# Moving the checks of sums and small norm steps from GpSimd to VectorE, and the bias add into an accumulating DMA

## The chip, the cores and the metric

The kernel runs on one core of a Trainium2 chip. The metric is the device time of one execution in microseconds (us). The engines are PE (TensorE, matmuls), DVE (VectorE), ACT (ScalarE), POOL (GpSimd) and SP (SyncE); each works through its own instructions in program order and waits for others through semaphores. DMAs are issued from SP and from POOL.

## The reference

Two layers of a transformer over graphs with 16 graphs (b), 1024 nodes and 256 features. Each layer computes h = relu(layernorm(x)), then masked attention over h, and adds the result to x. The first layer has 4 heads of 64, the second 8 heads of 32 and biases on its projections:

```python
h = jnp.maximum(_layernorm(x, axis=-1), 0.0)
scores = jnp.einsum('bhne,bhme->bhnm', Q, K) * scale
scores = jnp.where(mask, scores, -jnp.inf)
attn = jax.nn.softmax(scores, axis=-1)
heads = jnp.einsum('bhnm,bhme->bhne', attn, V)
x = x + concat @ Wo.T + bo
```

The mask comes from an integer adjacency matrix of 1024 x 1024 for each b. All arithmetic is float32.

## The kernel before, in words

The whole work of both layers is one stream of steps, whose order is written out by the program itself. A layer of one b has two halves of 512 query rows (qh) and two groups of heads (g) in each; a group is 4 steps in the first layer and 8 in the second, so that there are 768 steps in all. The first layer of element b+1 stands in the stream ahead of the second layer of element b. A step computes four blocks of scores, 128 keys by 512 queries each, in two PSUM pairs of tiles: `scores` (PE, L372); then for each pair the mask is put on by a minimum (DVE, L388) and the exponential is taken (ACT, L393). Two steps later `weigh` multiplies with the values (PE, L405). Three PSUM pairs are shared by the scores, the projections (`kq` L212, `values` L241), the transposes (`turn` L200) and the output projection (`end_half` L353).

The sums of the exponentials are formed in two ways. In the first layer, `add_tiles` adds a step's tiles on DVE or POOL (L416) and to the running sum on POOL (L418). In the second layer, POOL adds the tiles of two successive steps in place (`count_steps`, L502). A matmul with ones (L278) then sums over the keys.

After the last step of a group its sums go through a fixed set of calls that are due some steps later. `spread` brings them by two small DMAs into `sn`, a tile of 128 lanes by 8 (first layer) or 16 elements. `invert` takes the reciprocal on DVE (L305) and brings it back by DMAs as `inv`. `test`, one step after `invert`, checks on POOL that each sum lies between 1e-15 and 1e15 and multiplies the outcome into the tile `chk` (L318, L319). `normalize` multiplies on POOL (L324), and `end_half` projects and adds to x (DVE, L358). At the end of the program `chk` decides whether a slower, careful program has to run.

The norms are prepared beside the stream: `stats` takes mean and variance on DVE (L165, L166), then four small POOL operations give `rstd` and `shift` (L169 to L175); `norm` applies them on ACT (L182); `add_bias`, a step after the last part of `norm`, adds the output bias `bo` to the rows of x on POOL (L190), long before `end_half` adds the projected attention to the same rows. The functions due in a step are called after that step's exponentials, so that on DVE and POOL they stand between the masking of this step and that of the next; those in the set LARGE and `turn` come last. The adjacency rows are loaded by casting DMAs that POOL issues (L126), transposed by SP's DMAs (L130), and changed in place on DVE for the second layer (`second`, L144).

Of the kernel before, what the change touches and what calls it, by code (L numbers as in the profile page):

```python
# [10 lines left out]
F32 = mybir.dt.float32  # L11
# [4 lines left out]
ALU = mybir.AluOpType  # L16
PSUM = bass.MemoryType.PSUM

P = 128
EPS = 1e-5  # L20
# [62 lines left out]
def fast_program(ctx, tc, a, w, loads, chk):  # L83
# [3 lines left out]
    nc = tc.nc  # L87
    x, adj, out = a["x"], a["adj"], a["out"]
    B, N, E = x.shape
# [8 lines left out]
    small = ctx.enter_context(tc.tile_pool(name="small", bufs=4))  # L98
# [50 lines left out]
    class Inputs:  # L149
# [6 lines left out]
        def stats(self, half, tiles=range(4)):  # L156
            n = f"{self.n}_{half}"
            if 0 in tiles:
                self.mv[half] = small.tile([P, 4, 2], F32, tag="mv", name=f"mv_{n}")
            mv = self.mv[half]  # L160
            for i in tiles:
                stats = small.tile(
                    [P, nc.vector.BN_STATS_DIM], F32, tag="stats", name=f"st_{n}_{i}"
                )
                nc.vector.bn_stats(stats, xs[self.b, half][:, i, :])  # L165
                nc.vector.bn_aggr(mv[:, i, :], stats)  # L166
            if 3 in tiles:
                ve = small.tile([P, 4], F32, tag="ve", name=f"ve_{n}")
                nc.gpsimd.tensor_scalar_add(ve, mv[:, :, 1], EPS)  # L169
                self.rstd[half] = small.tile([P, 4], F32, tag="rstd", name=f"rstd_{n}")  # L170
                nc.gpsimd.tensor_tensor(self.rstd[half], ve, w.mhalf, ALU.pow)
                less = small.tile([P, 4], F32, tag="less", name=f"less_{n}")
                nc.gpsimd.tensor_scalar_mul(less, mv[:, :, 0], -1.0)
                self.shift[half] = small.tile([P, 4], F32, tag="shift", name=f"shift_{n}")
                nc.gpsimd.tensor_mul(self.shift[half], less, self.rstd[half])  # L175

# [10 lines left out]
        def add_bias(self, half):  # L187

            rows = xs[self.b, half]
            nc.gpsimd.tensor_add(  # L190
                rows, rows, w.bo[self.layer].unsqueeze(1).to_broadcast([P, 4, E])
            )

        def turn(self, half):
# [56 lines left out]
    class Group:  # L251
# [62 lines left out]
        def test(self):  # L314
            c = chk[:, : self.n_f]
            for bound, op in ((SUM_MIN, ALU.is_ge), (SUM_MAX, ALU.is_le)):
                ok = small.tile([P, self.n_f], F32, tag="ok", name=f"ok_{self.n}_{op.name}")
                nc.gpsimd.tensor_scalar(ok, self.sn, bound, 1.0, op0=op, op1=ALU.mult)  # L318
                nc.gpsimd.tensor_mul(c, c, ok)  # L319

        def normalize(self):
            if self.g == 0:
# [301 lines left out]
    for b in range(B - 1):  # L624
        mine, a, c = inputs[1][b], first[b + 1], second[b]
# [284 lines left out]
```

## Time and profile before

| | |
|---|---|
| Median of 3 runs (lowest to highest) | 3377.39 us (3377.24 to 3378.44) |
| The profiled execution, its span | 3380.06 us, 3378.3 us |
| Granted TensorE clock | 0.998 |
| Busy: PE, DVE, POOL, ACT | 99%, 74%, 72%, 65% |
| DMA queue of POOL: packets, MB, share of 16 engines | 18432, 33.56, 6.3% |
| DMA queue of SP | 232080, 105.18, 12.6% |

A line of the timeline has the start in us, the length in us, the engine, the line of the kernel, the operation and the tiles that it writes and reads, and in brackets the idle time of the engine just before it with what ended it; neighbours of one kind are merged, and x counts them. A line of the groups has the busy time in us, the mean length in ns, and the idle time before. The ends of matmuls are modelled, so PE is better read from the starts of its instructions.

### The profile page before, as it was taken

The page shows a single profiled execution, that of the slowest core. Times are in us where ns is not written, and L with a number is a line of the kernel's source. Part 1 is how long each engine was busy: PE and PEld are TensorE (multiplying, and loading weights), DVE is VectorE, ACT ScalarE, POOL GpSimd, SP SyncE. Part 2 cuts the span into 40 slices and gives each one's busy share as a digit, 9 for nine tenths or more (in the row PEclk, how much of TensorE's full clock was granted, in tenths as well). Part 3 has the DMA queues.
Part 4 walks back from the last instruction along what each step waited for, and adds up shares of the span by engine and source line. Part 5 has one row for each costly group of instructions (what it writes and reads, how often), then busy time and mean ns, then how long its engine had stood idle before and what let it go on. Part 6 is the DMA issues. An engine that isn't in the chain of part 4 may idle for free. (4 is left out here: it accounts for less than half of the span.)

```text
span 3378.3 us, 46298 instructions
## 1 busy us (share of the span) xinstructions
PE 3339.0 (99%) x18190; PEld 1298.6 (38%) x18190; DVE 2501.1 (74%) x2664; ACT 2182.5 (65%) x2402; POOL 2447.1 (72%) x1606
## 2 busy tenths in 40 slices
PE   8999999999999999999999999999999999999998
PEld 3443333333333333333334333333343333433432
DVE  4676767767677786777867778677786777777876
ACT  5567566675666756667566675666756667665665
POOL 5577778777677766877677686777867778676776
PEclk9999999999999999999999999999999999999999
DMA  6221111212112111121221212212121111210001
GB/s 131 48 42 36 48 39 36 51 36 47 36 36 51 42 42 36 39 48 42 45 39 36 48 39 48 39 39 45 39 47 37 48 39 36 51 38 18 14 17 31
DMA packets 250738, 141.77 MB, mean 42 GB/s; under 512 B 182416, under 2 KB 217488, under 8 KB 250512
## 3 DMA queue, kind: packets, MB, share of 16 engines
q1 hardware_dynamic: 232080, 105.18, 12.6%
q0 software_dynamic: 18432, 33.56, 6.3%
q8 instruction: 144, 2.36, 0.3%
q14 instruction: 82, 0.67, 0.1%
HBM read 120.33 MB, written 18.34 MB: 41 GB/s over the span
## 5 line engine op out<-in xcount | busy, mean ns | idle before, releaser
L393 ACT ACTIVATE p<-p 128x1024 f32<-128x1024 f32 x1536 | 1615.1, 1057 | 973.8 <-DVE p L388 931.7
L388 DVE SCALAR_TENSOR_TENSOR p<-mask,ps 128x1024 f32<-128x1024 fp8e4 x1536 | 1797.0, 1215 | 583.5 <-PE ps L372 553.8
L502 POOL TENSOR_TENSOR p<-p,p 128x2048 f32<-128x2048 f32 x255 | 1161.9, 4557 | 372.2 <-PE po L405 368.3
L372 PE MATMUL ps<-qT,kT 32*128 32x512 f32 (+1 forms) x6144 | 1145.6, 631 | 7.6 <-DVE p L388 4.9
L405 PE MATMUL po<-p,v 128*32 128x512 f32 (+1 forms) x6144 | 992.4, 601 | 0.4 <-ACT o L288 0.4
L418 POOL TENSOR_TENSOR t<-t,t 128x1024 f32<-128x1024 f32 x192 | 486.2, 2532 | 389.8 <-DVE t L416 341.6
L372 PEld LDWEIGHTS ps<-qT,kT 32*128 32x128 f32 (+1 forms) x6144 | 367.7, 184 | 675.7 <-issue 305.3
L405 PEld LDWEIGHTS po<-p,v 128*32 128x32 f32 (+1 forms) x6144 | 227.8, 118 | 689.4 <-issue 529.1
L416 DVE TENSOR_TENSOR t<-p 128x1024 f32<-128x1024 f32 x192 | 325.0, 1693 | 14.6 <-POOL t L418 14.4
L278 PE MATMUL pz<-p,ones 128*32 128x512 f32 x2056 | 267.8, 593 | 0.2 <-POOL p L502 0.2
L212 PE MATMUL pq<-hT,wk 128*128 128x512 f32 x512 | 240.7, 613 | 3.1 <-ACT hT L201 3.1
L353 PE MATMUL py<-wo,cat 128*128 128x256 f32 x1008 | 237.8, 387 | 4.7 <-POOL cat L324 2.8
L241 PE MATMUL pv<-wv,hT 128*128 128x256 f32 x1024 | 237.9, 385 | 0.1
L212 PE MATMUL pq<-hT,wq 128*128 128x512 f32 x512 | 236.6, 605 | 0.0
L241 PEld LDWEIGHTS pv<-wv,hT 128*128 128x128 f32 x1024 | 189.4, 190 | 71.7 <-issue 24.0
L353 PEld LDWEIGHTS py<-wo,cat 128*128 128x128 f32 x1008 | 185.4, 190 | 80.0 <-issue 33.4
L324 POOL TENSOR_TENSOR cat<-o,inv 128x512 f32<-128x512 f32 x127 | 164.5, 1296 | 10.3 <-DMA inv<-vd 9.3
L416 POOL TENSOR_TENSOR t<-p 128x1024 f32<-128x1024 f32 x64 | 165.0, 2578 | 2.8 <-ACT p L393 2.4
L358 DVE TENSOR_TENSOR x<-py,x 128x1024 f32<-128x1024 f32 x63 | 76.4, 1213 | 118.4 <-PE py L353 118.4
L190 POOL TENSOR_TENSOR x<-x,bo 128x1024 f32<-128x1024 f32 x64 | 152.6, 2385 | 1.5 <-DMA bo<-in_bo_dram 1.4
L212 PEld LDWEIGHTS pq<-hT,wk 128*128 128x128 f32 x512 | 93.5, 192 | 145.2 <-issue 120.1
L212 PEld LDWEIGHTS pq<-hT,wq 128*128 128x128 f32 x512 | 92.2, 189 | 139.8 <-issue 138.3
(51 smaller groups left out, 1635.4 us busy)
## 6 DMA issues: line engine op xcount, KB each, us to landing
adj<-in_adj_dram POOLq DMA_DIRECT2D x128, 256.0 KB, 3.6
x<-in_x_dram SPq DMA_DIRECT2D x32, 512.0 KB
inv<-vd SPq DMA_DIRECT2D x128, 128.0 KB
inv<-vd SPq DMA_DIRECT2D x252, 64.0 KB
out_dram<-x SPq DMA_DIRECT2D x31, 512.0 KB
adjT<-adj SPq DMA_TRANSPOSE x128
sd<-s SPq DMA_DIRECT2D x64, 4.0 KB
sn<-sd SPq DMA_DIRECT2D x64, 4.0 KB
```

Source lines behind the costliest of these rows:

```text
L212: nc.tensor.matmul(pq[:, m, :], wt[self.layer][:, c, ts(m, P)], self.hT[half][:, c, :], start=(c == 0), stop=(c == 1),)
L241: nc.tensor.matmul(pv[:, i, :], self.hT[half][:, c, ts(i, P)], w.v[self.layer][:, c, :], start=(c == 0), stop=(c == 1),)
L278: nc.tensor.matmul(self.s[r * self.D : (r + 1) * self.D, :], w.ones[:, : self.D], p[:, r, :], start=start, stop=stop,)
L324: nc.gpsimd.tensor_mul(self.half.cat[:, self.g, :], self.ob, self.inv)
L353: nc.tensor.matmul(py[:, i, :], self.half.cat[:, c, ts(i, P)], w.o[self.layer][:, c, :], start=(c == 0), stop=(c == 1),)
L372: nc.tensor.matmul(st.ps[i // 2][:, i % 2, :], gr.inp.kT[r * D : (r + 1) * D, gr.g, ts(kt, P)], gr.inp.qT[r * D : (r + 1) * D, gr.g, ts(gr ...
L388: nc.vector.scalar_tensor_tensor(out=half, in0=gr.mask.m[:, kt, ts(gr.qh, 512)].unsqueeze(1).to_broadcast([P, 2, 512]), scalar=BIG, in1=st ...
L393: nc.scalar.activation(half, half, AF.Exp, scale=gr.scale)
L405: nc.tensor.matmul(gr.o[r * D : (r + 1) * D, :], gr.inp.v[:, kt, h * D : (h + 1) * D], st.p[:, i, :], start=(kt == 0), stop=(kt == NT - 1),)
L416: engine.tensor_add(t, st.p[:, 0:2, :], st.p[:, 2:4, :])
L418: nc.gpsimd.tensor_add(t, t, gr.t)
L502: nc.gpsimd.tensor_add(one, one, st.p)
```

## The change

The four operations of `test` for a group become two on DVE, each of which compares `sn` with a bound and multiplies the outcome into `chk`; the tiles `ok` go. In `stats`, the addition of EPS and the negation of the mean go from POOL to DVE; the power and the product stay on POOL. In `add_bias`, POOL issues a DMA that adds the bias, repeated for four row tiles, to the rows of x in SBUF.

```diff
             if 3 in tiles:
                 ve = small.tile([P, 4], F32, tag="ve", name=f"ve_{n}")
-                nc.gpsimd.tensor_scalar_add(ve, mv[:, :, 1], EPS)
+                nc.vector.tensor_scalar_add(ve, mv[:, :, 1], EPS)
                 self.rstd[half] = small.tile([P, 4], F32, tag="rstd", name=f"rstd_{n}")
                 nc.gpsimd.tensor_tensor(self.rstd[half], ve, w.mhalf, ALU.pow)
                 less = small.tile([P, 4], F32, tag="less", name=f"less_{n}")
-                nc.gpsimd.tensor_scalar_mul(less, mv[:, :, 0], -1.0)
+                nc.vector.tensor_scalar_mul(less, mv[:, :, 0], -1.0)
...
         def add_bias(self, half):
 
             rows = xs[self.b, half]
-            nc.gpsimd.tensor_add(
-                rows, rows, w.bo[self.layer].unsqueeze(1).to_broadcast([P, 4, E])
+            nc.gpsimd.dma_start(
+                rows, w.bo[self.layer].unsqueeze(1).to_broadcast([P, 4, E]), accum_op=ALU.add
             )
...
         def test(self):
             c = chk[:, : self.n_f]
             for bound, op in ((SUM_MIN, ALU.is_ge), (SUM_MAX, ALU.is_le)):
-                ok = small.tile([P, self.n_f], F32, tag="ok", name=f"ok_{self.n}_{op.name}")
-                nc.gpsimd.tensor_scalar(ok, self.sn, bound, 1.0, op0=op, op1=ALU.mult)
-                nc.gpsimd.tensor_mul(c, c, ok)
+                nc.vector.scalar_tensor_tensor(
+                    out=c, in0=self.sn, scalar=bound, in1=c, op0=op, op1=ALU.mult
+                )
```

## The prediction

> **What bounds the kernel now.** I read the page's busy shares first, then the groups, then every gap between the starts of consecutive matmuls, then the timeline around the places where the moved instructions stand.
>
> ```profile
> PE 3339.0 (99%) x18190; PEld 1298.6 (38%) x18190; DVE 2501.1 (74%) x2664; ACT 2182.5 (65%) x2402; POOL 2447.1 (72%) x1606
> ...
> L502 POOL TENSOR_TENSOR p<-p,p 128x2048 f32<-128x2048 f32 x255 | 1161.9, 4557 | 372.2 <-PE po L405 368.3
> ...
> L416 DVE TENSOR_TENSOR t<-p 128x1024 f32<-128x1024 f32 x192 | 325.0, 1693 | 14.6 <-POOL t L418 14.4
> ...
> L190 POOL TENSOR_TENSOR x<-x,bo 128x1024 f32<-128x1024 f32 x64 | 152.6, 2385 | 1.5 <-DMA bo<-in_bo_dram 1.4
> ```
>
> PE is the bound, and not only by its modelled busy time. In the gaps between starts I find the same distance for the same pair of lines again and again, and an excess over it of 28.4 us in all: 11.4 before 100 us, 5.1 after 3200 us, and about 0.78 us in each of the 208.4 us periods between (one batch element each). So at most some 28 us can be gained, and in the steady state 0.78 a period. DVE and POOL have idle time but stand in strict order: what they delay reaches PE once its slack is gone.
>
> The second thing to see is that DVE and POOL exclude each other. The tensor_tensor of L416 has a mean of 1693 ns, though undisturbed it takes 1.22 us; here it starts during a POOL add:
>
> ```profile
> 420.32 2.38 POOL L416 TENSOR_TENSOR t<-p 128x1024 f32<-128x1024 f32 x1
> 420.48 3.32 DVE L416 TENSOR_TENSOR t<-p 128x1024 f32<-128x1024 f32 x1
> ```
>
> POOL ends at 422.70, DVE at 423.80: DVE waited for POOL's end and then took 1.1 us. And once, late in the run, such a wait reaches PE:
>
> ```profile
> 3211.27 4.54 POOL L502 TENSOR_TENSOR p<-p,p 128x2048 f32<-128x2048 f32 x1 [0.24 <-PE po L405]
> ...
> 3212.40 3.96 DVE L144 TENSOR_SCALAR mask<-mask 128x1024 fp8e4<-128x1024 fp8e4 x1
> ...
> 3216.28 3.47 DVE L388 SCALAR_TENSOR_TENSOR p<-mask,ps 128x1024 f32<-128x1024 fp8e4 x3
> ...
> 3217.55 1.13 PE L372 MATMUL ps<-qT,kT 32*128 32x512 f32 x4 [2.10 <-DVE p L388]
> ```
>
> L144 normally takes 0.69 us. Blocked by L502 until 3215.81 it takes 3.96, the masking L388 behind it is late, and PE stands still for 2.1 us.
>
> [...] L388 reads one SBUF tensor and PSUM, and its 1536 times lie between 1159 and 1224 ns. [...] Here the 256 KB adj DMAs occupy POOL for 527 to 773 ns and land after 3.6 us.
>
> **The change part by part.** POOL loses 64 x 2.385 us (L190), 256 small operations of L318 and L319 (some 1.25 us a group with gaps) and two small ones a norm. It gains 64 DMA issues. DVE gains two two-input operations a group (256) and two tensor_scalar a norm (128). I price each of these at 0.15 us, below the 0.17 to 0.25 us of the small reciprocal L305: 384 x 0.15 = 58 us of 877 us DVE idle time. As busy time this is nothing. What counts is that each check now waits on DVE for POOL's current instruction, with the L388 pair of the next step queued behind it, then ACT's exponentials and PE. I go through one period with DVE's order written out.
>
> Site A, second layer's second group, its check comes at 1146.96, right after the norm statistics:
>
> ```profile
> 1140.91 4.56 POOL L502 TENSOR_TENSOR p<-p,p 128x2048 f32<-128x2048 f32 x1 [3.95 <-PE po L405]
> ...
> 1145.41 0.59 POOL L126 DMA_DIRECT2D adj<-in_adj_dram  x1
> ...
> 1146.08 0.27 POOL L318 TENSOR_SCALAR ok_is_ge<-sn 128x16 f32<-128x16 f32 x1
> ...
> 1146.78 0.18 DVE L166 BATCH_NORM_AGGREGATE mv<-st 128x2 f32<-128x6 f32 x1
> 1146.88 2.33 DVE L388 SCALAR_TENSOR_TENSOR p<-mask,ps 128x1024 f32<-128x1024 fp8e4 x2
> ...
> 1147.27 4.55 POOL L502 TENSOR_TENSOR p<-p,p 128x2048 f32<-128x2048 f32 x1
> ...
> 1149.27 3.07 PE L241 MATMUL pv<-wv,hT 128*128 128x256 f32 x13
> ```
>
> With L318 and L319 off POOL, the next L502 starts at 1146.07 instead of 1147.27 (its inputs are ready: it overwrites a tile that PE read last by 1144.49) and ends at 1150.62. The check, ready at 1146.96, waits 3.7 us; with two operations of 0.15 the L388 pair is 4.0 late. That pair ends at 1149.21 and PE takes the freed PSUM pair at 1149.27: slack 0.06. PE loses 3.95 us. The place recurs 14 times: **55 us**.
>
> Site B, fourth group, check behind the L388 that ends at 1176.15:
>
> ```profile
> 1170.58 4.60 POOL L502 TENSOR_TENSOR p<-p,p 128x2048 f32<-128x2048 f32 x1
> ...
> 1173.79 4.62 DVE L388 SCALAR_TENSOR_TENSOR p<-mask,ps 128x1024 f32<-128x1024 fp8e4 x4 [1.51 <-PE ps L372]
> ...
> 1175.11 2.45 POOL L190 TENSOR_TENSOR x<-x,bo 128x1024 f32<-128x1024 f32 x1
> ```
>
> Before, L190 stands at 1168.26 and 1175.11, and L502 follows at 1178.84. If a bias DMA occupies POOL as an adj issue does (0.62 us), the first L502 starts at about 69.0, the second at 74.9 and blocks the check from 76.1 to 79.5: 3.7 us late, slack 1.67 (freed at 1177.28, used at 1178.94), 2.05 us lost, 14 times: **29 us**. If the issue takes over about 1.57 us the check slips in ahead: nothing. The trace has no accumulating DMA; 512 pieces of 1 KB against 128 rows of an adj load could cost up to four times 0.62, so the bounds are 0.6 and 2.5 us, and I take the low end.
>
> Site C, first layer's last group, 1076.50: L502 runs to 1079.62, DVE was idle until 1077.70 and has slack 1.71; 0.57 us, 14 times: **8**. Site D, 1063.49: two norm operations and two checks in a row, slack 0.2 after a gap of 0.2, and the pow L171 (1.04) may get in between: 0 to 1.3 us, I take 0.5, 14 times: **7**. The other tensor_scalar pairs: one meets an L502 for about 2.2 us with slack 1.73[...]: 0 to 0.6, I take 0.3: **4**. The remaining four checks of a period fall into DVE idle time of 1 to 5 us (at 1021, 1042, 1114, 1207): nothing; without that cover each could cost up to one POOL add, 2.4 or 4.6 us. After 3200 us, where L502 runs almost without pause, five checks lose about 2.2 each: **11**.
>
> POOL's relief brings: L324 is late for PE's L353 by 0.38 us once a period behind L318 and L319, with 0.16 at the next L372: 0.55, 15 times: **-8**. The opening norm chain may be 0.5 us shorter, or later if its order turns out worse; taken at nothing. Of the DMA: 33.5 MB more on a queue that now takes 6.3% of the engines; x is needed again many steps later (L358), which hides landing. It could slow the small transfers to sn, on which DVE waits 43.5 us in all: 0 to 14 us, taken at nothing because round trip and use are 1 to 3 us apart. POOL's pow now waits for DVE's ve; behind it stand L324 and L502, which mostly wait for PE anyway.
>
> Sum: 55 + 29 + 8 + 7 + 4 + 11 - 8 = 106 us. The profiled execution took 3380.06 (span 3378.3 and 1.8 around it), 2.7 above the median 3377.39; nothing in the difference matters at this size. 3377 + 106 = 3483, given as **3480**.
>
> **Rivals.** (1) The issue is long: site B goes, 3454. For it speak the 512 pieces; it is inside the main case. (2) The block is worse: second check also behind an add, D and the pairs at their high ends, shifted POOL adds meeting L416 and L144: some 40 us more, 3525. (3) No block for operations of 8 or 16 elements[...]: then only 0.3 us a period is added at A against 0.55 regained: 3374, no change. Against it speaks POOL's own L318 of 8 elements, which takes up to 1119 ns instead of 253 beside a DVE L416. (4) Faster: POOL's relief takes effect[...]. It decides at A, from a wait under 0.06 us: 8 us of the period stalls and up to 6 of the opening go: 3363. (5) The accumulation is carried out in more pieces or with a wait of POOL for its landing (3.6 us or more, 64 times): POOL would lose more than L190 costs, sites shift, 3400 to 3500.
>
> **How the numbers follow.** About 0.2% (6.8 us) is what a measurement of this kernel can tell from no change. Blocking, with or without site B, and (5): 0.88, all slower. No change: 0.07. Faster: 0.05. The range 3400 to 3525 runs from A at half its size with the gains to the high ends.
>
> **What would show it.** Right: the check's operations on DVE with a median near 0.15 us but a maximum of 3 to 4.6 us; L372 or L241 with idle time put down to L388; stalls of about 4 us every 208 us; DVE idle time down; POOL without L190. Wrong: maxima under 0.5 us, or an unchanged period of 208.4 us. A long POOL time for the bias DMA would show rival 1.

## The result, and the profile after

The changed kernel takes 3577.14 us (median of 4 runs, 3572.55 to 3577.28) against 3377.38 us: a ratio of 1.0587, interval 1.0569 to 1.0606, 200 us more. The forecast was 3480 us with a range up to 3525. The direction held, the size was about half. The profiled execution has a span of 3575.3 us, 197.0 more than before.

These lines of the profile after answer to those shown of before (three dots stand for lines left out). In a busy line each engine has its busy time, its share of the span and its number of instructions; a group has busy time, mean ns of one, and idle time before it with what ended it; a DMA issue has the KB of one and the us to landing.

```profile
PE 3435.9 (96%) x18190; PEld 1328.1 (37%) x18190; DVE 2762.4 (77%) x3048; ACT 2183.9 (61%) x2402; POOL 2192.2 (61%) x966
...
L502 POOL TENSOR_TENSOR p<-p,p 128x2048 f32<-128x2048 f32 x255 | 1175.7, 4611 | 633.9 <-PE po L405 617.6
L372 PE MATMUL ps<-qT,kT 32*128 32x512 f32 (+1 forms) x6144 | 1205.6, 644 | 104.1 <-DVE p L388 97.8
...
L416 DVE TENSOR_TENSOR t<-p 128x1024 f32<-128x1024 f32 x192 | 282.7, 1473 | 2.4 <-POOL t L418 2.0
...
L317 DVE SCALAR_TENSOR_TENSOR chk<-sn,chk 128x8 f32<-128x8 f32 (+1 forms) x256 | 242.6, 948 | 4.4
...
x<-bo POOLq DMA_DIRECT2D x64, 512.0 KB, 6.4
```

POOL lost 255 us of busy time, and gained as much idle time behind PE. The checks L317, 8 or 16 elements each, have a mean of 948 ns, 242.6 us in all. L372 now stands idle for 104.1 us, of which 97.8 were ended by the mask L388, which stands on DVE behind the checks. Before, it was 7.6 us in the whole run:

```profile
L372 PE MATMUL ps<-qT,kT 32*128 32x512 f32 (+1 forms) x6144 | 1145.6, 631 | 7.6 <-DVE p L388 4.9
```

The line of all checks together shows that the mean is made of two kinds (min/median/max):

```profile
L317 DVE SCALAR_TENSOR_TENSOR chk<-sn,chk x256: 134/174/3937, 90.5 to 3565.5; 128x8 f32<-128x8 f32 x64, 128x16 f32<-128x16 f32 x64
```

At site A the timeline runs as the forecast said. (Start and length in us; x2 merges the two checks.)

```profile
1192.71 0.58 POOL L126 DMA_DIRECT2D adj<-in_adj_dram  x1
...
1193.31 4.55 POOL L502 TENSOR_TENSOR p<-p,p 128x2048 f32<-128x2048 f32 x1
...
1194.18 3.93 DVE L317 SCALAR_TENSOR_TENSOR chk<-sn,chk 128x16 f32<-128x16 f32 x2
...
1198.03 2.35 DVE L388 SCALAR_TENSOR_TENSOR p<-mask,ps 128x1024 f32<-128x1024 fp8e4 x2
...
1199.30 2.08 PE L372 MATMUL ps<-qT,kT 32*128 32x512 f32 x4 [3.15 <-DVE p L388]
...
1201.31 5.30 PE L241 MATMUL pv<-wv,hT 128*128 128x256 f32 x16
```

L502 follows the adj issue at once, the checks become ready at 1194.18 and end with L502, and PE stands still until the mask is done. What the forecast did not have is in the last two lines. Before, four matmuls of L372 are shown with 1.13 or 1.14 us and 13 of L241 with 3.07; here four take 2.08 and 16 take 5.30. The starts of L241 lie 427 ns apart instead of 216. The windows give the reason: after the length of a window and the busy times of PE, PEld, DVE, ACT and POOL stands the granted TensorE clock, then the DMA share and GB/s.

```profile
1192.00:1199.00 7.00, 4.14 (x28) 1.03 (x26) 6.90 (x9) 2.12 (x2) 5.84 (x3) 0.91 0.53 112
1199.00:1206.00 7.00, 6.70 (x18) 4.40 (x19) 5.90 (x14) 4.23 (x4) 2.47 (x3) 0.61 0.00 0
1206.00:1212.00 6.00, 6.00 (x46) 2.05 (x45) 4.12 (x7) 3.98 (x6) 3.15 (x1) 1.00 0.01 3
```

From 1197.70 to 1204.53, for 6.83 us, the trace has the clock at one half; then it is full again. In the whole run such stretches last 184.9 us (32 of them, all but two of 3.41 or 6.83 us), before 16.9 us (3); the last one of each run reaches 2.0 us past the last instruction. The mean granted clock fell from 0.998 to 0.974.

Both kernels issue the same 18190 matmuls, in the same order but for four near the end, so each gap between two starts can be set against the same gap of before. The excess, summed by place, is split in two: what matmul work lost in half-clock stretches (half of their overlap), and the rest, which is standing still.

| Place (forecast's name) | forecast | standing still | half clock |
|---|---|---|---|
| A, second layer's second group, 14 times | 55 | 52.9 | 37.2 |
| B, its fourth group, 14 times | 29 | 35.1 | 12.6 |
| C, first layer's last group, 15 times | 8 | 16.2 | 2.9 |
| D | 7 | 1.8 | 0 |
| norms' tensor_scalars | 4 | 12.4 | 0 |
| after 3190 us | 11 | 25.0 | 13.3 |
| relief of POOL | -8 | -16.3 | 0 |
| opening and rest | 0 | 1.0 | 2.9 |
| sum | 106 | 128.1 | 68.9 |

The two measured columns make up the 197.0. (Where a stretch begins within a standstill the split is good to some us.)

### The profile page after: what moved, and what is told of

It is laid out like the page before. It is cut to its first block, busy times and chain, and to the rows that moved or that the text cites. A ratio compares the mean times of both kernels' runs of the same rounds, so it can differ in the third digit from the quotient of the medians.

```text
span 3575.3 us, 46236 instructions
## 1 busy us (share of the span) xinstructions
PE 3435.9 (96%) x18190; PEld 1328.1 (37%) x18190; DVE 2762.4 (77%) x3048; ACT 2183.9 (61%) x2402; POOL 2192.2 (61%) x966
## 3 DMA queue, kind: packets, MB, share of 16 engines
q0 software_dynamic: 52224, 67.12, 12.7%
## 5 line engine op out<-in xcount | busy, mean ns | idle before, releaser
L388 DVE SCALAR_TENSOR_TENSOR p<-mask,ps 128x1024 f32<-128x1024 fp8e4 x1536 | 1796.9, 1214 | 587.6 <-PE ps L372 586.8
L502 POOL TENSOR_TENSOR p<-p,p 128x2048 f32<-128x2048 f32 x255 | 1175.7, 4611 | 633.9 <-PE po L405 617.6
L372 PE MATMUL ps<-qT,kT 32*128 32x512 f32 (+1 forms) x6144 | 1205.6, 644 | 104.1 <-DVE p L388 97.8
L405 PE MATMUL po<-p,v 128*32 128x512 f32 (+1 forms) x6144 | 1006.0, 609 | 3.9 <-ACT p L393 3.3
L372 PEld LDWEIGHTS ps<-qT,kT 32*128 32x128 f32 (+1 forms) x6144 | 376.3, 186 | 809.1 <-issue 314.9
L416 DVE TENSOR_TENSOR t<-p 128x1024 f32<-128x1024 f32 x192 | 282.7, 1473 | 2.4 <-POOL t L418 2.0
L241 PE MATMUL pv<-wv,hT 128*128 128x256 f32 x1024 | 263.6, 415 | 0.0
L317 DVE SCALAR_TENSOR_TENSOR chk<-sn,chk 128x8 f32<-128x8 f32 (+1 forms) x256 | 242.6, 948 | 4.4
L241 PEld LDWEIGHTS pv<-wv,hT 128*128 128x128 f32 x1024 | 207.7, 208 | 87.2 <-issue 24.0
L353 PE MATMUL py<-wo,cat 128*128 128x256 f32 x1008 | 236.0, 387 | 2.2 <-DVE p L388 2.2
L353 PEld LDWEIGHTS py<-wo,cat 128*128 128x128 f32 x1008 | 187.5, 191 | 73.7 <-issue 34.1
L324 POOL TENSOR_TENSOR cat<-o,inv 128x512 f32<-128x512 f32 x127 | 171.5, 1350 | 24.0 <-DMA inv<-vd 23.3
L136 ACT ACTIVATE mask<-adjT,mhalf 128x1024 fp8e4<-128x1024 bf16 x128 | 145.2, 1136 | 6.1 <-DMA adjT<-adj 6.0
```

Source lines behind the costliest of these rows:

```text
L241: nc.tensor.matmul(pv[:, i, :], self.hT[half][:, c, ts(i, P)], w.v[self.layer][:, c, :], start=(c == 0), stop=(c == 1),)
L317: nc.vector.scalar_tensor_tensor(out=c, in0=self.sn, scalar=bound, in1=c, op0=op, op1=ALU.mult)
L353: nc.tensor.matmul(py[:, i, :], self.half.cat[:, c, ts(i, P)], w.o[self.layer][:, c, :], start=(c == 0), stop=(c == 1),)
L372: nc.tensor.matmul(st.ps[i // 2][:, i % 2, :], gr.inp.kT[r * D : (r + 1) * D, gr.g, ts(kt, P)], gr.inp.qT[r * D : (r + 1) * D, gr.g, ts(gr ...
L388: nc.vector.scalar_tensor_tensor(out=half, in0=gr.mask.m[:, kt, ts(gr.qh, 512)].unsqueeze(1).to_broadcast([P, 2, 512]), scalar=BIG, in1=st ...
L405: nc.tensor.matmul(gr.o[r * D : (r + 1) * D, :], gr.inp.v[:, kt, h * D : (h + 1) * D], st.p[:, i, :], start=(kt == 0), stop=(kt == NT - 1),)
```

## The experiments

The theory: DVE operations with a second SBUF input wait for POOL's current instruction (a check takes up to 3.94 us, with a median of 0.17), the mask behind them is late, PE stands still, and a standstill that is long enough costs a stretch at half clock as well. Rivals: DVE's place for the checks is the trouble (order, number of operations), not a wait for POOL; the clock drops come from something else in the changed kernel; the loss comes from the DMA or the norms.

**1. The form of the operation.** The changed kernel, with each check made of two DVE operations with one SBUF input, at the same place:

```diff
-            for bound, op in ((SUM_MIN, ALU.is_ge), (SUM_MAX, ALU.is_le)):
-                nc.vector.scalar_tensor_tensor(
-                    out=c, in0=self.sn, scalar=bound, in1=c, op0=op, op1=ALU.mult
-                )
+            at = next(places)
+            for k, op in enumerate((ALU.min, ALU.max)):
+                nc.vector.tensor_reduce(
+                    ends[:, k, at : at + 1], self.sn, mybir.AxisListType.X, op
+                )
```

The minima and maxima of all groups are compared with the bounds once, at the end.

> The whole change, but each check is two DVE tensor_reduce operations (least and greatest sum of a lane into a column of its own), with one SBUF input each, and the bounds are applied once at the end[...]. As many DVE operations at the same places as in the change. Theory 1[...]: no operation over 0.4 us, no stall at A, B and C, clock at full, 3365 to 3385 us. Rival (the added DVE work, or its place in DVE's order): 3540 or more.

Measured: 3384.46 us, ratio 1.0020 (1.0012 to 1.0029). As many operations at the same place, 193 us less. All 256 of the new ones are short:

```profile
L320 DVE TENSOR_REDUCE ends<-sn x256: 127/153/164, 92.2 to 3374.4; 128x1 f32<-128x8 f32 x64, 128x1 f32<-128x16 f32 x64
```

So it is not the move to DVE, nor the number or the place of the operations, but their form. The mask L388 points to the second SBUF input as what matters in it: it is a scalar_tensor_tensor as well, reads one tensor in SBUF and one in PSUM, and all its 1536 times in the changed kernel lie between 1160 and 1223 ns. One SBUF input alone does not free an operation of the wait, though: the tensor_scalar of `ve` has one, and in experiment 2 it takes up to 2.48 us, against 0.17 at its shortest. Why a tensor_reduce with one does not wait is not shown.

**2. The checks alone, and all but the checks.** The first is the kernel before with only the edit of `test`, the second the changed kernel with `test` back on POOL.

> Of the change only the checks of sums go to DVE; the norm operations stay on POOL and the bias is added by POOL's tensor_add. Theory 1 (a check waits at three places of a period for POOL's add, PE runs dry, and after the longer stalls PE's clock is granted at half): most of the loss, but not all, because the tensor_add of 2.4 us holds the next add back at site B, so that the check there goes first: 14 x (2.4 stall + about 1.1 of clock) less, 3500 to 3540 us. Rival (the accumulating DMA costs the time, by its traffic and its issue): 3380 to 3400. Rival (the added DVE work itself, 256 small operations of 0.17 us): under 3425.

> The change without its checks: these stay on POOL, the norm operations are on DVE and the bias is added by DMA. Theory 1: 3370 to 3385 us, with the addition of EPS still blocked for about 2 us once a period and 0.2 us of it reaching PE. Rival (the DMA): 3500 or more.

Measured: 3662.13 us for the checks alone, 1.0841 (1.0823 to 1.0859), far above what I expected; 3401.94 us for the rest, 1.0076 (1.0060 to 1.0093), 17 above the range given. Both misses have a cause that the traces show. The timeline of the checks alone, at site B:

```profile
1254.26 2.40 POOL L190 TENSOR_TENSOR x<-x,bo 128x1024 f32<-128x1024 f32 x1
...
1255.20 5.95 DVE L317 SCALAR_TENSOR_TENSOR chk<-sn,chk 128x16 f32<-128x16 f32 x2
...
1256.60 4.52 POOL L502 TENSOR_TENSOR p<-p,p 128x2048 f32<-128x2048 f32 x1
...
1262.34 2.08 PE L372 MATMUL ps<-qT,kT 64*128 64x512 f32 x4 [4.08 <-DVE p L388]
```

The first check waits 1.5 us for the bias add L190; POOL starts L502 as that ends, before the second check has begun; the second waits 4.4 more. Two dependent small operations in a row can each be caught by an operation of its own. At B this kernel stands still for 61.8 us and loses 37.0 to the clock, at C 46.1 and 16.5. In the changed kernel, where POOL issues a DMA instead of the add, B and C of the same 14 periods together come to 60.4 instead of 161.4. So the accumulating DMA, taken at nothing in the forecast, saves the checks some 100 us. (This is read from the timelines of both sites, where an L190 catches one of the two checks; no run has the checks with the DMA and without the norms' edit.)

In the kernel without the checks, `ve` is what is late (its operation has 4 elements, read at a stride of two):

```profile
525.47 4.54 POOL L502 TENSOR_TENSOR p<-p,p 128x2048 f32<-128x2048 f32 x1
...
528.54 1.50 DVE L169 TENSOR_SCALAR ve<-mv 128x4 f32<-128x4 f32 x1
...
534.72 4.55 POOL L502 TENSOR_TENSOR p<-p,p 128x2048 f32<-128x2048 f32 x1 [2.05 <-PE po L405]
...
536.81 2.48 DVE L169 TENSOR_SCALAR ve<-mv 128x4 f32<-128x4 f32 x1
```

It is caught twice a period, and each time L388 stands right behind it. Measured by place: 15.5 and 12.9 us of standstill, against 9.8 us of relief. With the checks on DVE only the second is left, since L502 then starts some 1.2 us earlier and the first `ve` finds POOL free (0.17 us).

**3. The DMA alone and the norms alone**, each put into the kernel before, to see which of the two that loss comes from.

> The kernel before, with the bias added by the accumulating DMA, and nothing else changed. If the 1.1 us a period that the change without its checks lost are DVE's ve (L169) meeting L502 twice a period, this kernel has none of it: 3370 to 3380. If they come from the DMA (slower transfers, POOL held by the issue): 3390 to 3397.

> The kernel before, with ve and less on DVE. The change without its checks lost 1.15 us a period, the DMA alone gained 1.0; so if the two norm operations alone are the loss, with ve (L169) waiting for L502 twice a period, they cost 2.15 us a period: 3377 + 14 x 2.15 = 3407. If the loss is a product of both edits (L502 moved by the DMA into ve's place): 3377 to 3390.

Measured: the DMA alone 3373.36 us, 0.9985 (0.9979 to 0.9992), a gain of 1.0 us a period; the norms alone 3412.92 us, 1.0101 (1.0086 to 1.0116), a loss of 2.15 a period. The first lies in the range of the theory of `ve`, the second 6 us above its figure; the loss is the norms', not the DMA's. The DMA is cheap for DVE but not free for POOL, as the timeline of the DMA alone shows:

```profile
1163.60 4.57 POOL L502 TENSOR_TENSOR p<-p,p 128x2048 f32<-128x2048 f32 x1 [1.92 <-PE po L405]
1168.10 1.39 POOL L190 DMA_DIRECT2D x<-bo  x1
1169.01 5.11 POOL L502 TENSOR_TENSOR p<-p,p 128x2048 f32<-128x2048 f32 x1
1173.53 1.85 POOL L190 DMA_DIRECT2D x<-bo  x1
```

An issue occupies POOL for 1.3 to 1.9 us, and the L502 behind it can take 5.11 instead of 4.57.

**4. One site back.** The changed kernel, with only site A's group checked on POOL as before.

```diff
+            pool = self.layer == 1 and self.qh == 0 and self.g == 1
             for bound, op in ((SUM_MIN, ALU.is_ge), (SUM_MAX, ALU.is_le)):
+                if pool:
...
+                    nc.gpsimd.tensor_scalar(ok, self.sn, bound, 1.0, op0=op, op1=ALU.mult)
+                    nc.gpsimd.tensor_mul(c, c, ok)
+                    continue
```

> The whole change, but the checks of one group of the second layer in four (first half of the rows, second group: site A) are on POOL as before. Theory 1: site A alone falls away, 14 times 3.3 us of stall and 3.4 us of half clock (6.8 us at half): 3577 - 94 = 3483, between 3465 and 3500. If the slower clock does not count: 3577 - 46 = 3531.

Measured: 3478.56 us, 1.0299 (1.0282 to 1.0316), 98.6 us less than the changed kernel. Half-clock stretches fall from 184.9 to 55.0 us. One place out of eight groups holds half of the loss. The difference by place is A's own 90.1 us, less 15.5 for the first `ve`, which is caught again, and 18 us after 3190 us, where the group comes once more (experiment 6 shows what its check does there); the other places differ by a few us.

**5. Is it the standstill that costs the clock?** A delay without a wait for POOL: the kernel before, with DVE maxima over a v tile (one SBUF input) at site A. The half dose is one maximum over 1024 values (1.19 us), the single dose one over 2048 (2.25 us), the double dose two of these.

```diff
+            if self.layer == 1 and self.qh == 0 and self.g == 1:
+                for k in range(2):
+                    nothing = small.tile([P, 1], F32, tag="nothing", name=f"nothing_{self.n}_{k}")
+                    nc.vector.tensor_reduce(
+                        nothing, self.inp.v, mybir.AxisListType.XY, ALU.max
+                    )
             c = chk[:, : self.n_f]
```

> The kernel before, with one DVE maximum over 1024 values at site A, half of the single dose: about 1.15 us of delay, 1 us of PE stall. Length alone: 14 us, 3391. If a stretch at half clock follows a stall of this length too: 1.7 us more each, 3415. I expect 3391: in the changed kernel stalls of 1 us and less left the clock alone.

> The kernel before, with one added DVE maximum over the 2048 values of a v tile at site A (14 to 16 times in the run), about 2.2 us, one SBUF input[...]: a pure delay of the L388 pair. If a stall costs only its length: 2.15 us x 14 = 30 us, 3407. If every stall is followed by a stretch at half clock (3.41 us, so 1.7 us lost at least): 3431. I take the first with few half-clock stretches, since the checks at sites C and B with stalls under 1.9 us showed few: 3409 (3400 to 3420).

> As the single dose, with two such maxima in a row at site A: 4.35 us of delay, about the 4 us that the blocked checks had there. Length alone: 4.35 x 14 = 61 us, 3438. With a stretch of 3.4 to 6.8 us at half clock after each stall, 1.7 to 3.4 us more: 3462 to 3486. Theory (the clock follows any stall of this length[...]): 3475. Rival (the clock drops come from something else in the changed kernel): 3438.

| | measured (ratio, interval) | standstill at A, 14 times | half clock at A |
|---|---|---|---|
| half dose | 3396.06 (1.0053, 1.0037 to 1.0068) | 15.6 | 0 |
| single dose | 3443.58 (1.0190, 1.0174 to 1.0205) | 29.2 | 30.5 |
| double dose | 3485.97 (1.0315, 1.0299 to 1.0331) | 60.1 | 35.8 |

The windows after the standstill, for the half, the single and the double dose in turn, have the clock (third number from the end) at 1.00, 0.61 and 0.50:

```profile
313.00:317.00 4.00, 4.00 (x17) 2.85 (x18) 3.93 (x7) 2.79 (x3) 3.82 (x3) 1.00 0.34 66
```

```profile
313.00:317.00 4.00, 4.00 (x11) 2.64 (x12) 3.93 (x7) 2.80 (x3) 3.01 (x6) 0.61 0.34 66
```

```profile
317.00:321.00 4.00, 4.00 (x11) 2.20 (x8) 3.93 (x8) 2.72 (x4) 1.97 (x5) 0.50 0.00 0
```

The standstill grows with the dose by its length alone, as expected (14, 30 and 61 us). The clock comes as a step: nothing after 1.1 us, a stretch of 3.41 us or more after 2 us, 6.83 us after 4.3. For the single dose I had bet on length alone, 3409; there the rival at 3431 was nearer, and it too was short, because some of the stretches last 6.83 us. The double dose lies at the top of its 3462 to 3486, 11 us above the bet. The rival that the drops come from something else in the changed kernel falls.

I counted all standstills above 0.7 us between 100 and 3330 us (on the clock of before) in before, the changed kernel, the checks alone, one site back and the three doses. They are measured between the starts of matmuls, which gives some 0.5 us more than the brackets of the timeline. Of 47 up to 1.75 us, 5 have a half-clock stretch in them or within 3.5 us after; of 73 from 1.75 to 2.75 us, 45; of 65 longer ones, all.

**6. A version that beats both.** The reduced checks without the other two edits, the reduced checks with the DMA, and that with two exceptions: the last element's second layer is checked on POOL, and the first element's first-layer bias is added on POOL.

> The kernel before, with each check made of a minimum and a maximum over sn on DVE (one SBUF input each), bounds applied once at the end; norms and bias as before. No DVE operation of these waits for POOL, and POOL is relieved of 256 small operations: 3365 to 3376. If the reductions do wait for L190 or L502 after all when the bias add is on POOL: 3450 or more.

> Checks as minimum and maximum over sn on DVE, the bias by the accumulating DMA, norms on POOL as before. Each of the two alone shortens the period, by 0.69 and 1.0 us. If they add up: about 3360 less some us lost at 3200 to 3300: 3364. If both regain the same stalls (L324 late for L353): 3370 to 3374.

> Reduced checks and the accumulating DMA as in the kernel before this one, but the four groups of the last element's second layer checked on POOL and the first element's first-layer bias added on POOL, as before the change. The period should again be 1.5 us shorter than before; if the 7.6 us lost before 310 us and the 7.1 us lost after 3000 us came from those two places, 3357 to 3362; if they come from chance in the loads and from the shifted phase of L502 against L144, 3365 to 3374.

Measured: 3375.45 us (0.9989, 0.9983 to 0.9996), 3373.71 us (0.9983, 0.9975 to 0.9991) and 3367.42 us (0.9968, 0.9956 to 0.9980). The periods get shorter as expected, by 0.7 and by 1.5 us, so the two reliefs add up in steady state. The second kernel gave most of its 20 us back at the ends: 7.6 us before 310 us and some 7 us after 3000 us, among these a standstill of 3.1 us near 3225 with half clock behind it that before did not have. So its time falls into the band for reliefs that do not add up, though in the periods they do. With the two exceptions the profiled execution is 1.9 us ahead of before at 310 us, but still loses 7.4 after 3000 us: the end's loss did not come from the last element's checks.

The record shows where it does come from. Before, the four POOL operations of one check of the last element but one keep two L502 apart, and the last mask change of `second` (L144) runs between them:

```profile
3224.65 4.56 POOL L502 TENSOR_TENSOR p<-p,p 128x2048 f32<-128x2048 f32 x1 [8.84 <-PE po L405]
...
3229.53 0.69 DVE L144 TENSOR_SCALAR mask<-mask 128x1024 fp8e4<-128x1024 fp8e4 x1
...
3230.90 4.55 POOL L502 TENSOR_TENSOR p<-p,p 128x2048 f32<-128x2048 f32 x1
```

Without them the second L502 follows at once and the mask change is caught, here in the last kernel (its L517, L147 and L387 are L502, L144 and L372):

```profile
3204.74 9.06 POOL L517 TENSOR_TENSOR p<-p,p 128x2048 f32<-128x2048 f32 x2 [10.53 <-PE po L420]
...
3209.63 4.73 DVE L147 TENSOR_SCALAR mask<-mask 128x1024 fp8e4<-128x1024 fp8e4 x1
...
3215.70 2.08 PE L387 MATMUL ps<-qT,kT 32*128 32x512 f32 x4 [3.02 <-DVE p L403]
```

In all six kernels with this check on DVE, in whatever form, that operation takes 4.7 us; in all eight with it on POOL, one site back among them, 0.69. The last kernel put the checks of the wrong element back.

3367.42 beats before by 0.3% and lies in the slower of its two expected bands. That the opening gained by the edit and not by chance is not settled, since runs of the second kernel spread from 3367.92 to 3376.13. What a minimum or maximum makes of a sum that is not a number was not tried.

## Why the prediction went wrong in size

**What failed is the price of a standstill.** The forecast wrote "PE loses 3.95 us. The place recurs 14 times: 55 us". The standstill measured 52.9 us: its length, its place, its cause and its number of times were right. But I priced it by its length, as though PE resumed at full speed. Each of the 14 standstills at A had a stretch of 3.41 or 6.83 us at half clock with it, another 37.2 us at A and 68.9 in all: three quarters of the 91 us by which 197 exceeds 106. Experiment 5 shows this without any of the change's edits. The rest, 22 us, is standing still that was mis-sized term by term, by -8 to +14 us in the table: that 128 lies near 106 is in part luck, since errors cancel.

The profile of before had it. These two windows, in the same columns, hold one of the opening's longest waits (PE waits 2.04 us until 65.51) and what follows:

```profile
62.00:66.00 4.00, 1.96 (x9) 0.68 (x6) 3.41 (x4) 4.00 (x6) 3.12 (x5) 1.00 0.82 130
66.00:70.00 4.00, 4.00 (x7) 1.64 (x6) 0.15 (x1) 3.38 (x5) 3.97 (x4) 0.57 0.40 72
```

I had counted the doubled gaps that follow into the "11.4 before 100" as if they were stalls. And the one late stall that I did look at, 2.10 us at 3217.55, has no half clock after it; it lies in the band where both happen (of 73 standstills from 1.75 to 2.75 us, 45 have one).

Point by point, in the order of the forecast:

- **DVE waits for POOL, L388 behind it, then PE.** Right; experiment 1 settles it.
- **Site A, 55.** Right in standstill (52.9), missing 37.2 of clock.
- **Site B, 29, decided by whether the issue takes less than 1.57 us.** 35.1 and 12.6. The issue measured 1.30 to 1.89 us, 1.84 at 1228.00, and yet the check did not slip in ahead: the profile has the next L502 from 1229.45, before the end of the issue, and the check only at 1230.56. Rival 1 falls: the issue was long in the sense of the forecast, but issue time and POOL's adds overlap in part, so that only 0.87 us lie between the end of one L502 (1228.58) and the start of the next.
- **Site C, 8.** 12.7 in the 14 periods: PE waits there for both pairs of the late L388, 0.9 us in sum, and I had counted one at 0.57. A 15th time, near 3309, both checks are caught (3.4 and 2.5 us), which costs 6.5 with its half clock.
- **Site D, 7.** 1.8, near the low end of its bounds.
- **Norms, 4.** 12.4. The tensor_scalar does wait for an L502, 2.18 us once a period, and the L388 behind it is late for both pairs, net 0.75 us.
- **The tail, 11.** 25.0 and 13.3: five checks wait 3.4 to 3.5 us where I took 2.2, and the second check of each is caught too, for 1.2 us by L324. The longest standstill there, 4.22 us until 3398.19, is not a check's in the main: L144 waits as in experiment 6, 4.73 us from 3390.92, and a check adds 1.2.
- **Relief, -8.** -16.3: the 0.38 us of L353 as foreseen, and 1.04 us a period at the L372 behind it where I had 0.16.
- **The DMA at nothing.** Right for its landing (6.4 us, nothing waited for it); wrong by omission, since it takes a 2.4 us add out of the way of the checks at two sites.

The rivals: "the block is worse" (3525) named the second check behind an add, which the checks alone show and the changed kernel mostly does not, and shifted POOL adds meeting L144, which happened once, in the tail. No rival had a cost that comes after the wait, so the range ended at 3525.

## What to carry to other kernels

When PE is the bound, price a new wait in front of it by its length and by the clock that it may cost: here nothing after the 1.1 us of the half dose, and 1.7 to 3.4 us more after most standstills of about 2 us (45 of 73) and after all 65 longer than 2.75, so the granted clock in windows around a stall of the profile before belongs into the working. Small operations put on DVE beside a busy POOL should have a form that does not wait: here 256 tensor_reduce over one SBUF tensor took 164 ns at most (experiment 1), while a scalar_tensor_tensor with two took up to 3.94 us in the changed kernel and a tensor_scalar with one (`ve`) up to 2.76 with the norms alone. The right form, for as many operations at the same place, was worth 193 us. Work taken off POOL can move POOL's long adds forward, onto a DVE operation that used to run before them, one that the change does not touch included (L144 in experiment 6, 4.73 us instead of 0.69).

## What was not expected of the hardware

- Of the 32 half-clock stretches of the changed kernel 12 last 3.41 us, 18 last 6.83 and one 10.24 (from 3518.76); the last one of the run is recorded with 10.80. How long a standstill must be for one is not a point: up to 1.75 us 5 of 47 had one, from 1.75 to 2.75 us 45 of 73, above that all 65.
- An add on POOL (L502) just after the issue of an accumulating DMA takes up to 5.14 us instead of 4.56, in 28 places of the changed kernel and in none of before. Whether the transfer or the issue slows it is open.
- An operation of 4 elements (`ve`) waited up to 2.76 us for POOL (norms alone); a check of 16 elements once 7.2 us (checks alone, from 2156.34): it outlasted the rest of an L190, a whole L502 and an L324. So one operation can wait for more than POOL's current instruction.
